# The norms of a four-layer graph kernel: who adds epsilon, who takes the power, who makes the shift

## The chip, the cores and the metric

The kernel runs on one core of one Trainium2 chip. The metric is device microseconds of one launch. A run of the kernel as it stands takes 2153.46 us in the median of three runs (2152.71 to 2155.54). The program's instructions are written out at compile time; nothing in their order is decided on the chip.

## What is computed

There are 128 graphs of 64 nodes with 256 features each, and one 64x64 adjacency matrix shared by all of them. Four layers follow each other, and each begins with a norm:

```python
for layer in (L0, L1, L2, L3):
    m = mean(x, -1);  v = var(x, -1)
    h = maximum((x - m) / sqrt(v + 1e-5), 0)
    x = x + layer(h, adj, weights)
```

- L0 has two graph products with a dense layer each, then four LSTMs over windows of 1, 2, 3 and 4 nodes.
- L1 has a graph product, attention with 4 heads of 64, a feed-forward part, and three more norms inside: after the graph product, after the attention and at the end.
- L2 is a graph attention layer. L3 works in the eigenbasis of the normalised Laplacian, so the kernel also decomposes a 64x64 matrix.

## The kernel before

**Tiles.** The 8192 rows (128 graphs of 64 nodes) are 64 tiles of 128 rows. L0 runs in 8 groups of 8 tiles; the other three layers run in 16 groups of 4 tiles (`HT = 4`). Two 64-row graphs share a tile.

**Stages.** In the profile, L0's groups run from the start to about 1360 us, roughly 165 us each; the groups of L1 to L3 run from about 1364 us to the end, with up to eight of them open at once. The decomposition (vectors of 1 to 128 elements in the tile `arena`) runs beside L0 as background work for VectorE until about 1300 us.

**Who sets the order.** No engine's order is written by hand. The class `Plan` (line 69) records every operation, simulates the five engines with a price for each operation (`cost`, line 176), and lists the operations in the order in which the simulation started them (`schedule`, line 227). `issue` (line 338) then emits them, which is why all instructions carry line 344 in the profile. Each engine runs its own list strictly in that order; semaphores make it wait for the other engines. Four facts of the planner matter here:

- The price of a GpSimd power is 0.44 + 0.14 us an element, of other GpSimd work 0.12 + 0.00218 us an element (line 217). VectorE's tensor_scalar between two SBUF tensors is 0.075 + 0.0006 us an element, scalar_tensor_tensor 0.075 + 0.00105.
- Operations that the planner counts as using the port that VectorE and GpSimd share (`op.port`, line 159: all of GpSimd's, and VectorE's that touch SBUF alone, but not bn_stats, bn_aggr and reductions) are never started side by side in the simulation.
- Between ready operations of one engine, `rank` (line 328) decides. In L0, the norms of the next group (`plan.lead = 1`, line 1311) go ahead of the LSTMs of the current one.
- A different price or engine anywhere can change the order everywhere after it.

**The norm.** `ln_stats` (line 1195) takes the statistics of `n` tiles (4, or 2 in the first group): bn_stats and bn_aggr on VectorE for each tile, giving mean and variance, then four small operations on GpSimd for all `n` at once (lines 1204 to 1207): add 1e-5 to the variance, raise to the power -0.5, multiply the mean by that, negate. The results are a scale and a shift per row. ScalarE applies them in one activation per tile, either with a Relu (`relu_norm`, line 1509, and in `layer0`, line 1309) or without (`norm`, line 1498). All these small values live in one tile `stat`.

**How many.** L0 has 4 norms in its first group and 2 in each of the other 7, so 18. L1, L2 and L3 have 6 norms per group of 4 tiles (4 in `layer1`, line 1523, and 1 each in `layer2`, line 1598, and `layer3`, line 1632), and 16 groups, so 96. Together there are 114, which is also the number of powers in the profile.

**Other names.** `big` are 4-tile buffers (parts of `arena`, `sums`, `mids` and `Whh` become `big` buffers once L0 and the decomposition are done). `mids` are the short-lived buffers of L0's gates. `bank` are the eight PSUM banks. `mhalf` holds -0.5.

Of the kernel before, what the change touches and what calls it, by code (L numbers as in the profile page):

```python
# [8 lines left out]
ALU = mybir.AluOpType  # L9
# [923 lines left out]
def gnn_kernel(ctx: ExitStack, tc: tile.TileContext, a, out):  # L933
# [48 lines left out]
    PE, V, ACT, G, SP = (plan.proxy(e) for e in ("PE", "V", "ACT", "G", "SP"))  # L982
# [212 lines left out]
    def ln_stats(src, n=HT):  # L1195

        s = plan.value("stat")
        st = s[:, :6 * n].rearrange("p (t k) -> p t k", k=6)
        mv = s[:, 6 * n:8 * n].rearrange("p (t k) -> p t k", k=2)
        rs = s[:, 8 * n:10 * n].rearrange("p (k t) -> p k t", k=2)  # L1200
        for t in range(n):
            V.bn_stats(st[:, t, :], src[:, t, :])
            V.bn_aggr(mv[:, t, :], st[:, t, :])
        G.tensor_scalar(rs[:, 0, :], mv[:, :, 1], 1e-5, None, op0=ALU.add)
        G.tensor_tensor(rs[:, 0, :], rs[:, 0, :], mhalf[:, :n], op=ALU.pow)
        G.tensor_tensor(rs[:, 1, :], mv[:, :, 0], rs[:, 0, :], op=ALU.mult)
        G.tensor_scalar(rs[:, 1, :], rs[:, 1, :], -1.0, None, op0=ALU.mult)
        return lambda t: rs[:, 0, t:t + 1], lambda t: rs[:, 1, t:t + 1]


# [98 lines left out]
    def layer0(fetched):  # L1309
        x = fetched()  # L1310
        plan.lead = 1
        nl = 2 if plan.group == 0 else HT
        norms = [ln_stats(x[t // HT][:, t % HT:t % HT + nl, :], nl) for t in range(0, GT, nl)]
        ayT = [fm() for hf in range(2)]
        for t0 in range(0, GT, nl):
# [182 lines left out]
    def norm(t):  # L1498

        sc, bi = ln_stats(t)  # L1500
        for i in range(HT):
            ACT.activation(t[:, i, :], t[:, i, :], AF.Identity, scale=sc(i), bias=bi(i))
# [6 lines left out]
    def relu_norm(x):  # L1509
        sc, bi = ln_stats(x)  # L1510
        h = tm()
        for t in range(HT):
            ACT.activation(h[:, t, :], x[:, t, :], AF.Relu, scale=sc(t), bias=bi(t))
        return h
# [197 lines left out]
```

## Time and profile before

| what | value |
|---|---|
| median of three runs | 2153.46 us |
| the profiled execution's own time | 2151.09 us |
| span of that execution, first to last instruction | 2149.3 us |
| TensorE busy in the span | 2102.0 us (98%) |
| VectorE busy | 1796.7 us (84%), 7434 instructions |
| ScalarE busy | 1124.1 us (52%) |
| GpSimd busy | 708.4 us (33%), 1040 instructions |
| the 114 powers on GpSimd | 123.9 us, 1088 ns each |
| the 228 adds and negations beside them | 69.8 us, 307 ns each |
| the 114 multiplications, nearly all of them (110) | 28.8 us, 264 ns each |

Between the profiled execution's span and its own time lie 1.8 us. The profile calls the engines PE (TensorE), DVE (VectorE), ACT (ScalarE), POOL (GpSimd) and SP (the queue that starts transfers). Busy times are sums over the whole launch. As the stages differ much, the views by stretch of time tell more than the totals.

### The profile page before, as it was taken

What the parts mean: (1) busy time and instruction counts of PE and PEld (TensorE: products, weight loads), DVE (VectorE), ACT (ScalarE), POOL (GpSimd) and SP (SyncE); (2) the same over time, 40 slices, a digit from 0 to 9 for tenths busy, and PEclk for the clock granted to TensorE, in tenths of its full rate; (3) what the DMA queues carried; (4) which work ended last, traced back from release to release, by engine and by line L of the source; (5) the groups of instructions that cost most, each with busy time, mean ns of one, the idle gap of its engine ahead of it and who ended that gap; (6) DMA issues with size and microseconds to landing.
All of it is one profiled execution on the core that took longest, in us unless ns stands there. A gap on an engine that the chain in (4) does not pass through costs nothing.

```text
span 2149.3 us, 46200 instructions
## 1 busy us (share of the span) xinstructions
PE 2102.0 (98%) x16772; PEld 1665.0 (77%) x16772; DVE 1796.7 (84%) x7434; ACT 1124.1 (52%) x2465; POOL 708.4 (33%) x1040
## 2 busy tenths in 40 slices
PE   9999999999999999999999999999999999999998
PEld 6688688688778778778778788877777877887776
DVE  5788888888999999989989898767787789876787
ACT  3354354355345345345345444566667666665783
POOL 7211211310110110110110002696556657864353
PEclk9999999999999999999999999999999999999999
DMA  5000100100100100100000111200000100000001
GB/s 206 1 3 22 42 2 22 41 1 21 40 1 21 40 1 21 40 1 21 26 1 21 50 40 51 90 1 2 21 22 21 41 22 21 11 12 11 2 2 60
DMA packets 44868, 57.70 MB, mean 27 GB/s; under 512 B 8928, under 2 KB 38496, under 8 KB 44640
## 3 DMA queue, kind: packets, MB, share of 16 engines
q1 hardware_dynamic: 43536, 53.71, 7.6%
q8 instruction: 131, 2.15, 0.4%
q10 hardware_dynamic: 1104, 1.05, 0.2%
q14 instruction: 97, 0.79, 0.1%
HBM read 37.53 MB, written 16.78 MB: 25 GB/s over the span
## 4 chain that ended last, share of the span: by engine, by line
PE 79%; DVE 11%; POOL 3%; issue 3%; ACT 2%; DMA 2%; SPq 0%; DVEq 0%; ACTq 0%; POOLq 0%
PE bank L344 79%; DVE stat L344 3%; DVE arena L344 3%; DVE big L344 3%; POOL stat L344 2%; DVE mids L344 1%; DVE sums L344 1%; DMA big<-in_x_dram 1%; ACT big L344 1%; ACT mids L344 1%; POOL arena L344 0%; ACT arena L344 0%; POOL big L344 0%; DVE Whh L344 0%; SPq L344 0%
## 5 line engine op out<-in xcount | busy, mean ns | idle before, releaser
L344 PE MATMUL bank<-big,Wih 128*128 128x256 f32 (+3 forms) x2408 | 731.7, 426 | 14.7 <-DVE arena L344 6.9
L344 PEld LDWEIGHTS bank<-big,Wih 128*128 128x128 f32 x2408 | 440.3, 190 | 183.0 <-issue 100.2
L344 ACT ACTIVATE mids<-bank,bl 128x256 f32<-128x256 f32 (+3 forms) x528 | 274.8, 527 | 385.7 <-PE bank L344 383.3
L344 PE MATMUL bank<-big,Whh 128*128 128x256 f32 (+2 forms) x1692 | 448.0, 366 | 1.5 <-DVE big L344 1.4
L344 DVE TENSOR_TENSOR arena<-arena 64x21 f32<-64x21 f32 (+5 forms) x2253 | 372.3, 195 | 29.5 <-POOL arena L344 1.2
L344 PEld LDWEIGHTS bank<-big,Whh 128*128 128x128 f32 x1692 | 306.8, 190 | 40.6 <-issue 8.6
L344 PE MATMUL bank<-big,sums 128*128 128x168 f32 (+2 forms) x1472 | 263.8, 321 | 1.6 <-ACT big L344 1.5
L344 POOL TENSOR_SCALAR stat<-stat 128x4 f32<-128x4 f32 (+1 forms) x228 | 69.8, 307 | 514.0 <-DVE stat L344 499.2
L344 PEld LDWEIGHTS bank<-big,sums 128*128 128x128 f32 (+1 forms) x1472 | 220.5, 185 | 17.4 <-issue 3.4
L344 ACT COPY mids<-bank 128x168 f32<-128x168 f32 (+2 forms) x427 | 146.2, 364 | 151.9 <-PE bank L344 146.0
L344 DVE TENSOR_TENSOR big<-mids 128x512 f32<-128x512 f32 (+2 forms) x256 | 141.5, 562 | 33.9 <-ACT mids L344 30.7
L344 ACT ACTIVATE mids<-mids,bl 128x336 f32<-128x336 f32 (+3 forms) x192 | 102.1, 539 | 78.7 <-DVE mids L344 74.9
L344 DVE TENSOR_TENSOR mids<-bank,mids 128x168 f32<-128x168 f32 (+2 forms) x322 | 116.1, 368 | 25.1 <-PE bank L344 17.6
L344 DVE SCALAR_TENSOR_TENSOR arena<-arena 64x1 f32<-64x1 f32 (+15 forms) x565 | 124.3, 243 | 6.1 <-POOL arena L344 2.5
L344 POOL TENSOR_TENSOR stat<-stat,mhalf 128x4 f32<-128x4 f32 (+1 forms) x114 | 123.9, 1088 | 5.6
L344 ACT ACTIVATE mids<-big 128x256 f32<-128x256 f32 (+2 forms) x176 | 89.4, 510 | 62.7 <-DVE big L344 46.3
L344 POOL TENSOR_TENSOR big<-big 128x168 f32<-128x168 f32 (+1 forms) x30 | 21.4, 726 | 272.5 <-DVE arena L344 105.7
L344 DVE TENSOR_SCALAR arena<-arena 64x1 f32<-64x1 f32 (+8 forms) x533 | 102.4, 199 | 8.3 <-POOL arena L344 0.4
L344 DVE TENSOR_TENSOR big<-big,mids 128x256 f32<-128x256 f32 (+2 forms) x194 | 95.2, 492 | 9.7 <-ACT mids L344 8.5
L344 PE MATMUL bank<-Wih,big 128*128 128x256 f32 x384 | 94.1, 383 | 3.1 <-DVE big L344 0.9
L344 POOL TENSOR_TENSOR arena<-arena 64x1 f32<-64x1 f32 (+1 forms) x70 | 46.8, 669 | 145.9 <-ACT arena L344 105.8
L344 ACT ACT_TABLE_LOAD x55 | 70.6, 1283 | 35.9 <-PE bank L344 18.0
(371 smaller groups left out, 3747.9 us busy)
## 6 DMA issues: line engine op xcount, KB each, us to landing
big<-in_x_dram SPq DMA_DIRECT2D x30, 512.0 KB, 5.5
put<-big SPq DMA_DIRECT2D x16, 512.0 KB, 2.8
arena<-put SPq DMA_DIRECT2D x8, 512.0 KB, 6.6
out_dram<-arena SPq DMA_DIRECT2D x16, 256.0 KB, 2.3
Wih<-in_WihT_dram SPq DMA_DIRECT2D x3, 1024.0 KB, 11.9
Whh<-in_WhhT_dram SPq DMA_DIRECT2D x3, 1024.0 KB, 13.9
big<-put SPq DMA_DIRECT2D x5, 512.0 KB, 5.4
out_dram<-big SPq DMA_DIRECT2D x10, 256.0 KB, 2.2
```

The costliest lines, as they stand in the source:

```text
L344: getattr(self.engines[op.eng], name)(*map(real, args), **{k: real(a) for k, a in kw.items()})
```

## The change

In `ln_stats`, epsilon is added by VectorE, the power stays on GpSimd, and the shift is made by one VectorE operation, (mean x -1) x scale, in place of a multiplication and a negation on GpSimd.

```diff
         for t in range(n):
             V.bn_stats(st[:, t, :], src[:, t, :])
             V.bn_aggr(mv[:, t, :], st[:, t, :])
-        G.tensor_scalar(rs[:, 0, :], mv[:, :, 1], 1e-5, None, op0=ALU.add)
+        V.tensor_scalar(rs[:, 0, :], mv[:, :, 1], 1e-5, None, op0=ALU.add)
         G.tensor_tensor(rs[:, 0, :], rs[:, 0, :], mhalf[:, :n], op=ALU.pow)
-        G.tensor_tensor(rs[:, 1, :], mv[:, :, 0], rs[:, 0, :], op=ALU.mult)
-        G.tensor_scalar(rs[:, 1, :], rs[:, 1, :], -1.0, None, op0=ALU.mult)
+        V.scalar_tensor_tensor(rs[:, 1, :], mv[:, :, 0], -1.0, rs[:, 0, :], op0=ALU.mult, op1=ALU.mult)
         return lambda t: rs[:, 0, t:t + 1], lambda t: rs[:, 1, t:t + 1]
```

The way from statistics to scale and shift was VectorE, GpSimd, ScalarE. It is now VectorE, GpSimd, VectorE, ScalarE, so VectorE's list holds an operation that waits for GpSimd. As the planner prices the new operations differently, it may put everything in another order.

## The prediction

> **What bounds the kernel now.** I read the shares of the engines first, then the busy times by stretch, then who TensorE waits for, and last the instructions around the places where it waits.
>
> ```profile
> PE 2102.0 (98%) x16772; PEld 1665.0 (77%) x16772; DVE 1796.7 (84%) x7434; ACT 1124.1 (52%) x2465; POOL 708.4 (33%) x1040
> ```
>
> TensorE lacks only 2149.3 - 2102.0 = 47 us of the span. By stretch (columns: stretch, length, then busy time and count of PE, PEld, DVE, ACT, POOL):
>
> ```profile
> 600.00:900.00 300.00, 296.11 (x1619) 237.60 (x1620) 279.87 (x1269) 137.69 (x312) 28.91 (x44) 1.00 0.07 22
> ...
> 1700.00:1900.00 200.00, 197.00 (x2217) 157.15 (x2216) 168.22 (x479) 137.85 (x257) 136.03 (x178) 1.00 0.06 18
> ...
> 2100.00:2149.30 49.30, 39.39 (x671) 33.38 (x669) 34.23 (x103) 17.79 (x35) 17.65 (x25) 0.97 0.16 55
> ```
>
> In the first layer VectorE is 93% busy and GpSimd 10%; later VectorE is at 84% and GpSimd at 68%; only in the last 50 us does TensorE stand for 10 us. So no gain of more than a few us is to be had but at the ends. The waits of TensorE from 60 to 1222 us:
>
> ```profile
> PE bank L344 <- DVE arena L344: 5.5, 5, 1.4
> PE bank L344 <- ACT mids L344: 2.7, 1, 2.7
> PE bank L344 <- DVE big L344: 2.2, 1, 2.2
> ```
>
> These 10.4 us are nearly all at six places, where one group of layer 0 ends and the next begins (227, 396, 563, 726, 890, 1052 us; 2.19, 1.41, 1.21, 1.21, 2.69, 1.21 us, sum 9.9). The fourth, from the timeline:
>
> ```profile
> 727.81 0.16 DVE L344 BATCH_NORM_AGGREGATE stat<-stat 128x2 f32<-128x6 f32 x1
> ...
> 728.06 0.23 POOL L344 TENSOR_SCALAR stat<-stat 128x4 f32<-128x4 f32 x1 [96.30 <-DVE stat L344]
> ...
> 728.37 1.04 POOL L344 TENSOR_TENSOR stat<-stat,mhalf 128x4 f32<-128x4 f32 x1
> ...
> 728.99 0.29 DVE L344 BATCH_NORM_AGGREGATE stat<-stat 128x2 f32<-128x6 f32 x2
> 729.20 1.26 DVE L344 TENSOR_TENSOR big<-mids 128x512 f32<-128x512 f32 x2
> ...
> 730.58 2.08 ACT L344 ACTIVATE mids<-big,stat 128x256 f32<-128x256 f32 x4
> 730.60 3.67 PE L344 MATMUL bank<-big,Wih 128*128 128x512 f32 x8 [1.21 <-DVE arena L344]
> ...
> 734.20 1.16 PE L344 MATMUL bank<-adjTb,mids 64*64 64x64 f32 x64
> ```
>
> The page blames "DVE arena", but what I read is this: VectorE spends 3.2 us on 8 bn_stats and 8 bn_aggr of the coming norms, and only then, at 729.20, makes the two LSTM products that give the gate buffers back; TensorE starts 0.14 us after they end (730.46). The norm's own user, the matmuls at 734.20, has no gap before it. At this place VectorE's time is dear and the norm's speed is worth nothing.
>
> **What the Trainium skill says.** "SBUF — State Buffer", section "Who interferes with whom": VectorE and GpSimd share a port pair; a VectorE instruction with two SBUF inputs, or a tensor_scalar in a two-port mode, and a GpSimd instruction block each other, whichever starts second waiting. Both new instructions are of these kinds. The trace agrees for VectorE: a tensor_scalar of 128x256 took 0.93 us at 2083.03, while GpSimd's 1.27 us addition from 2082.54 ran, and 0.28 us at 2102.96 with GpSimd idle. "TensorE: Matmul & The Clock Gate", section "Architectural detail: the array is 16× 32×32, not 1× 128×128", calls VectorE's queue strict FIFO: what waits at its head holds all behind it. The trace has no reordering on VectorE, but no wait for a norm's power in great number either, so it can't show the cost.
>
> **The change, part by part.** Each of 114 norms (18 in layer 0, 96 later) loses three GpSimd operations and gains two VectorE ones.
>
> *GpSimd.* Removed are 69.8 us of tensor_scalar (228) and about 30 us of multiplication (114 x 0.264): 100 of 708 us. Off TensorE's path, so worth nothing by itself.
>
> *VectorE's own time.* 4-element operations are not in the trace in these forms; the nearest rows are tensor_scalar 64x6 at 166 ns and scalar_tensor_tensor 64x1 at 189 ns. Back to back they take less: a bn_aggr of 155 ns lets the next start after 0.08 us, a dependent one follows after about 0.19 us (64x6 rows near 1228 us). So 0.08 to 0.19 us each; I take 0.15: 228 x 0.15 = 34 us, 5 of them in layer 0 and 29 later.
>
> *The latency of a norm.* Undisturbed, as at 2132 us, aggregation ends at 2132.01, the power starts at 2132.42, the negation ends at 2134.05: 2.04 us. After: eps add 0.17, hand-over 0.09 (as the aggregation at 6.75 to the addition at 6.84), power 1.04, hand-over 0.1, shift 0.19, hand-over as now: 1.6 to 1.7, so 0.35 saved. Where GpSimd is loaded, other additions now stand between power and negation (the median from the power's start to the negation's end is 1.88 us over the later layers, often 3 to 4); this too goes.
>
> *The wait.* The shift waits at the head of VectorE's list for the power. Nothing if the planner's clock is right (it prices the power at 1.00; 1.04 undisturbed, 1.10 mean), up to 1.04 us if VectorE arrives with the power just begun, more if GpSimd is behind. Behind it stand LSTM products, evacuations of PSUM, statistics, and so TensorE. The nearest row is layer 1's pass through GpSimd (multiply, add, maximum; 32 times):
>
> ```profile
> DVE sums L344 <- POOL sums L344: 10.6, 2, 9.4
> ...
> DVE sums L344 <- POOL stat L344: 0.9, 1, 0.9
> ```
>
> The first line is that pass, in which alone VectorE waits for such results there: 10.6 us for 32 passes, 0.33 us each, 0.04 without the longest. I take 0.3. (The second, 0.9 us, is all that VectorE waits for GpSimd's small statistics now.)
>
> *Layer 0, six places.* Ahead of the two LSTM products come now two epsilon additions and the first shift: 3 x 0.15 = 0.45 us, plus 0.05 of wait (the power starts about 728.2 and ends at 729.3, when VectorE has just finished the statistics). 6 x 0.5 = +3.0 us. Ends: 3 x 0.08 = 0.24 each, +1.4; and with one full wait of 1.04 each, +8.9; a gain is excluded, since nothing there stands waiting for a norm.
>
> *Later layers.* VectorE gains 29 us of work, 96 x 0.3 = 29 us of waits, and port holds: GpSimd's 128x512 additions take some 250 us of these 779 (a third), and an instruction that meets one waits half of its 1.3 us: 192 x 1/3 x 0.65 = 42 us. Together 100 us on an engine that is now idle for some 160. TensorE's waits put to VectorE from 1370 us to the end sum to 9.9 us, at about 615 us of VectorE work, 1.6%; as the margin shrinks I take 2%: 100 x 0.02 = +2.0 us. Ends: 0 if eight open groups cover it all, +10 if a tenth comes through; a gain, from the shorter latency, is the second rival.
>
> *The ends.* The last group's final three norms lie on the path: 3 x 0.35 = -1.0 us. When layers 1 to 3 begin (1370 to 1393 us), norms of several groups queue on GpSimd; TensorE lacks 1.6 us in 1380 to 1400; I take half, -0.8 us. In the first group transfers until 32 us cover everything: 0. If the last three norms lose their VectorE slot to other work, the -1.0 is gone.
>
> *Sum.* +3.0 + 2.0 - 1.0 - 0.8 = +3.2 us. The profiled execution took 2151.09 us (span 2149.3 and 1.8 around it), so 2154.3; the median is 2.4 higher, so 2153.46 + 3.2 = **2156.7 us**, +0.15%. A difference under 0.2%, 4.3 us, is about what a measurement of this kernel can't tell from none.
>
> **Rivals.**
> - *VectorE is held at its head.* The planner's list is right only while GpSimd keeps its time; under port conflicts powers take up to 1.99 us. A full 1.04 us at the six places (+8.9) and +4 later, less 1.8 at the ends: +11, **2164.6**. It speaks for it that VectorE is at 93% in layer 0, against it the 0.04 us of layer 1's usual pass. It decides where shifts wait over 0.5 us on average.
> - *The norms get faster, and it shows* (the other side). In the later layers a norm waits through GpSimd's list, and ScalarE waits 86 us there for it. If the shorter list closes half of the 25 us that TensorE lacks after 1370 us, -12, and layer 0 and VectorE's load cost +5: -7, **2146.5**. Against it: of these 25 us the trace puts only 0.8 directly to a norm on GpSimd. It decides where the stretch after 1370 us gains more than layer 0 loses.
> - *Nothing.* The new order happens to hide the added work at the six places: +0.5, **2154.0**.
>
> **Chances.** The sum's case 58% (own range 2152.5 to 2161.5: 30 points within 0.2%, 28 slower, as a new order moves it by some us either way), held VectorE 20% (slower), faster norms 16% (14 faster, 2 within), nothing 6% (within). Together 14% faster, 38% within, 48% slower. The range is 2149 to 2168: up to the held case and its spread, down to the upper half of the faster one; it leaves out about 2 in 10.
>
> **What would show it.** Right: TensorE's gaps at the six places longer by 0.3 to 0.6 us each, GpSimd about 100 us less busy, VectorE some 30 us more, waits of VectorE for "POOL stat" of 20 to 40 us where there were 0.9, aggregation to activation near 1.7 us at the last norm. Wrong: gaps at the six places unchanged, or TensorE's lack after 1370 us changed by over 5 us.

## The result, and the profile after

| | before | after |
|---|---|---|
| median of four runs each | 2153.54 us (2152.71 to 2155.54) | 2176.02 us (2175.23 to 2180.85) |
| ratio | | 1.0108, 95% interval 1.0094 to 1.0122 |
| the profiled execution's own time, and its span | 2151.09, 2149.3 us | 2175.5, 2173.7 us |

The change costs 22.5 us, 1.1%. The forecast was +3.2 us, with a range up to 2168: the sign of the likeliest case was right, the size was not. The page's shares of the engines, after:

```profile
PE 2103.6 (97%) x16772; PEld 1667.0 (77%) x16772; DVE 1837.8 (85%) x7662; ACT 1107.9 (51%) x2449; POOL 614.6 (28%) x698
```

GpSimd lost 93.8 us of work (about 100 were foreseen) and VectorE gained 41.1 (some 30 were). TensorE's work is unchanged (2103.6 against 2102.0), but it lacks 70.1 us of the span where it lacked 47.3. So the loss is standing time of TensorE. By stretch (columns as before; behind the engines stand the granted TensorE clock as a share of full speed, the busy share of the DMA engines and their GB/s):

```profile
600.00:900.00 300.00, 295.37 (x1613) 237.02 (x1611) 278.76 (x1275) 134.74 (x307) 20.26 (x28) 1.00 0.06 20
1700.00:1900.00 200.00, 189.85 (x2111) 151.16 (x2113) 174.53 (x530) 135.20 (x250) 110.72 (x98) 1.00 0.07 21
2100.00:2173.70 73.70, 59.75 (x1019) 50.67 (x1017) 56.82 (x195) 34.16 (x65) 22.17 (x20) 0.99 0.13 45
```

From 1700 to 1900 us TensorE lacks 10.2 us where it lacked 3.0, although VectorE is only at 87% there and GpSimd less busy than before.

**A cut that divides the loss.** The first transfer that belongs to the later layers (the profile shows it on SP's queue as arena<-put) starts at 1364.56 us before and at 1377.08 after. Up to it, both kernels do exactly the same matmuls, 8136. The busy times up to the cut, before and after (columns as above):

```profile
0.00:1364.56 1364.56, 1342.42 (x8136) 1061.76 (x8137) 1178.72 (x5666) 610.36 (x1515) 228.82 (x401) 1.00 0.09 29
```

```profile
0.00:1377.08 1377.08, 1344.29 (x8136) 1061.79 (x8137) 1187.80 (x5706) 610.98 (x1515) 209.60 (x341) 1.00 0.09 29
```

Layer 0 is 12.5 us longer: 10.7 of them TensorE stands (32.8 against 22.1), and 1.9 it spends on the same matmuls. The rest of the span is 796.6 us where it was 784.7, 11.9 longer, all of it standing. (The two make 24.4 us and not 22.5, since the profiled execution before lies 2.4 us under its median.) Layer 0 has 18 of the 114 norms and more than half of the loss, so the loss doesn't follow the number of norms.

**The first group.** From the timeline, the start before. The first norm is complete at 8.7 us and the first graph product starts at 9.38:

```profile
6.84 0.24 POOL L344 TENSOR_SCALAR stat<-stat 128x2 f32<-128x2 f32 x1 [4.84 <-DVE stat L344]
...
7.17 0.73 POOL L344 TENSOR_TENSOR stat<-stat,mhalf 128x2 f32<-128x2 f32 x1
...
8.72 1.09 ACT L344 ACTIVATE mids<-big,stat 128x256 f32<-128x256 f32 x2 [3.87 <-POOL stat L344]
...
9.38 1.41 PE L344 MATMUL bank<-adjTb,mids 64*64 64x64 f32 x32 [1.93 <-ACT mids L344]
```

And after:

```profile
8.49 0.43 DVE L344 BATCH_NORM_STATS2 stat<-big 128x6 f32<-128x256 f32 x1 [0.51 <-DMA big<-in_x_dram]
...
9.70 0.35 DVE L344 TENSOR_SCALAR stat<-stat 128x2 f32<-128x2 f32 x4
9.93 2.91 POOL L344 TENSOR_TENSOR stat<-stat,mhalf 128x2 f32<-128x2 f32 x4 [6.88 <-DVE stat L344]
...
12.96 0.15 DVE L344 SCALAR_TENSOR_TENSOR stat<-stat 128x2 f32<-128x2 f32 x1
...
13.15 2.57 ACT L344 ACTIVATE mids<-big,stat 128x256 f32<-128x256 f32 x5 [8.38 <-DVE stat L344]
...
13.80 2.50 PE L344 MATMUL bank<-adjTb,mids 64*64 64x64 f32 x68 [0.95 <-ACT mids L344]
```

The four epsilon additions ("x4" at 9.70) come together, behind the statistics of all eight tiles, and one of these waits for an input transfer. The first shift comes only at 12.96, and TensorE starts its first graph product 4.4 us later.

**The fourth of the six places**, where VectorE's list was thought to delay the two LSTM products:

```profile
734.40 0.67 DVE L344 TENSOR_TENSOR big<-mids 128x512 f32<-128x512 f32 x1
...
735.01 0.73 DVE L344 BATCH_NORM_STATS2 stat<-big 128x6 f32<-128x256 f32 x2
...
735.23 3.24 PE L344 MATMUL bank<-big,Wih 128*128 128x512 f32 x7 [1.56 <-DVE big L344]
```

The product now stands ahead of the statistics, so no addition and no shift can delay it, and still TensorE waits 1.56 us there (1.21 before) and another 1.40 at 742. This isn't the old order with two operations more; it is another order. Compared as lists, the matmuls of the two kernels differ from the first graph product on: 6609 of 16772 stand at the same place.

### The profile page after: what moved, and what is told of

The parts are those of the page before. It is cut to its first block, busy times and chain, and to the rows that moved or that the text cites. A ratio compares the mean times of both kernels' runs of the same rounds, so it can differ in the third digit from the quotient of the medians.

```text
span 2173.7 us, 45985 instructions
## 1 busy us (share of the span) xinstructions
PE 2103.6 (97%) x16772; PEld 1667.0 (77%) x16772; DVE 1837.8 (85%) x7662; ACT 1107.9 (51%) x2449; POOL 614.6 (28%) x698
## 4 chain that ended last, share of the span: by engine, by line
PE 80%; DVE 14%; DMA 2%; ACT 2%; issue 1%; POOL 1%; SPq 0%; DVEq 0%; ACTq 0%; POOLq 0%
PE bank L344 80%; DVE stat L344 4%; DVE arena L344 4%; DVE big L344 3%; DVE mids L344 2%; DVE sums L344 1%; DMA big<-in_x_dram 1%; ACT sums L344 0%; ACT big L344 0%; SPq L344 0%; POOL big L344 0%; ACT mids L344 0%; DMA Whh<-in_L_b_dram 0%; DMA arena<-put 0%; DMA Wg<-in_Wg_dram 0%
## 5 line engine op out<-in xcount | busy, mean ns | idle before, releaser
L344 PE MATMUL bank<-big,Wih 128*128 128x256 f32 (+3 forms) x2408 | 731.9, 426 | 19.1 <-DVE arena L344 10.7
L344 PE MATMUL bank<-big,Whh 128*128 128x256 f32 (+3 forms) x1948 | 452.7, 347 | 1.8 <-DVE big L344 1.7
L344 PEld LDWEIGHTS bank<-big,Whh 128*128 128x128 f32 (+1 forms) x1948 | 311.1, 183 | 40.6 <-issue 7.4
L344 POOL TENSOR_TENSOR stat<-stat,mhalf 128x4 f32<-128x4 f32 (+1 forms) x114 | 130.5, 1150 | 453.1 <-DVE stat L344 448.2
L344 PEld LDWEIGHTS bank<-big,sums 128*128 128x128 f32 (+1 forms) x1536 | 221.9, 183 | 15.8 <-issue 2.6
L344 ACT COPY mids<-bank 128x168 f32<-128x168 f32 (+2 forms) x400 | 131.7, 351 | 149.2 <-PE bank L344 145.9
L344 ACT ACTIVATE mids<-mids,bl 128x336 f32<-128x336 f32 (+2 forms) x192 | 102.1, 539 | 74.2 <-DVE mids L344 71.3
L344 PE MATMUL bank<-Wih,big 128*128 128x256 f32 x448 | 112.6, 386 | 6.4 <-ACT big L344 3.2
L344 ACT COPY big<-bank 128x512 f32<-128x512 f32 (+1 forms) x148 | 70.7, 506 | 63.9 <-PE bank L344 63.1
L344 PEld LDWEIGHTS bank<-Wih,big 128*128 128x128 f32 x448 | 82.5, 192 | 23.2 <-issue 4.6
L344 PE MATMUL bank<-Wih,sums 128*128 128x256 f32 x312 | 78.8, 388 | 5.4 <-ACT sums L344 2.7
## 6 DMA issues: line engine op xcount, KB each, us to landing
Wih<-in_WihT_dram SPq DMA_DIRECT2D x3, 1024.0 KB, 11.9
Whh<-in_WhhT_dram SPq DMA_DIRECT2D x3, 1024.0 KB, 13.9
```

The lines of the kernel that those rows point to most:

```text
L344: getattr(self.engines[op.eng], name)(*map(real, args), **{k: real(a) for k, a in kw.items()})
```

## The experiments

Three questions were put in turn: operations or order; where the order loses; and whether the order alone is enough. Each kernel ran beside the kernel before on the same chip, at 2153.4 to 2154.1 us in the median. "Standing" is TensorE's lack of busy time in the profiled span. Some expectations speak of the planner's own clock: that is the span with which its simulation ends, worked out as the program is compiled, and no measurement.

### Operations or order

**The new engines in the old order.** The planner records the four old operations and orders them as before; only when they are written out are the first and the last two replaced.

```diff
-                for name, args, kw in op.calls:
-                    getattr(self.engines[op.eng], name)(...)
+                for eng, name, args, kw in getattr(op, "emit", [(op.eng, *c) for c in op.calls]):
+                    getattr(self.engines[eng], name)(...)
...
         G.tensor_scalar(rs[:, 0, :], mv[:, :, 1], 1e-5, None, op0=ALU.add)
+        plan.ops[-1].emit = [("V", *plan.ops[-1].calls[0])]
         G.tensor_tensor(rs[:, 0, :], rs[:, 0, :], mhalf[:, :n], op=ALU.pow)
         G.tensor_tensor(rs[:, 1, :], mv[:, :, 0], rs[:, 0, :], op=ALU.mult)
+        plan.ops[-1].emit = []
         G.tensor_scalar(rs[:, 1, :], rs[:, 1, :], -1.0, None, op0=ALU.mult)
+        plan.ops[-1].emit = [("V", "scalar_tensor_tensor", ...)]
```

> The order is planned as before the change, with four GpSimd operations at their old prices; only when it is written out does the epsilon addition go to VectorE, at the addition's place in the order, and the shift as one VectorE operation, at the negation's place. The lists of TensorE, ScalarE and the DMA queue are those of before. If the two VectorE operations cost time by themselves (VectorE standing for the power, port holds), this is as slow as the change: 2170 to 2178 us. If the loss is that the planner wrote another order, it lies at 2150 to 2158 us. If both share it, 2160 to 2168 us.

Measured: 2162.96 us, ratio 1.0048 (1.0033 to 1.0063), +9.2. The profiled execution is its slowest, +13.8. Its VectorE stands 18.7 us in 20 waits for powers (total, times, longest):

```profile
DVE stat L344 <- POOL stat L344: 18.7, 20, 2.1
```

**The new order with the old engines.** The reverse: the planner orders the changed operations, and the old ones are written out (addition on GpSimd, and GpSimd's multiplication and negation in the place of the shift).

```diff
         V.tensor_scalar(rs[:, 0, :], mv[:, :, 1], 1e-5, None, op0=ALU.add)
+        plan.ops[-1].emit = [("G", *plan.ops[-1].calls[0])]
...
         V.scalar_tensor_tensor(...)
+        plan.ops[-1].emit = [("G", "tensor_tensor", ...), ("G", "tensor_scalar", ...)]
```

> The order is planned as after the change, but the epsilon addition is written out on GpSimd at its place, and at the place of the shift stand the multiplication and the negation on GpSimd. If the VectorE operations cost time by themselves, this falls back to 2150 to 2158 us, a few us more for GpSimd's operations standing where VectorE's were planned. If the other order is the loss, it stays at 2168 to 2178 us. If both share it, 2160 to 2168 us.

Measured: 2176.93 us, ratio 1.0109 (1.0092 to 1.0126), +23.2. All work is where it was before, and the whole loss is there. Its cut lies at 1376.05 us:

```profile
0.00:1376.05 1376.05, 1345.76 (x8136) 1064.91 (x8137) 1178.55 (x5666) 610.00 (x1515) 227.55 (x401) 1.00 0.09 29
```

The counts of VectorE and GpSimd (x5666, x401) are those of the kernel before; TensorE stands 30.3 us, as after the change (32.8). Its first graph product comes at 12.44 us, so the late start follows the order too. The order is enough to make the loss. The old operations stand here at places planned for others, though, and how much of the 23.2 us that adds isn't known.

**Each half in the old order.** Only the addition, or only the shift, is moved when written out (the first, or the last two, of the three lines above).

> In the order planned before the change, only the epsilon addition is written out on VectorE. If the direct loss of 9 us in the old order is VectorE's standing for the power and the port holds of the shift, this is 2153 to 2156 us. If VectorE's place for the addition (behind statistics that wait for a transfer, or held by GpSimd's port) is the loss, 2158 to 2163 us.

> In the order planned before the change, only the shift is written out on VectorE, at the negation's place. If VectorE's standing for the power and the port holds of the shift are the direct loss, 2159 to 2164 us. If the addition is, 2153 to 2156 us.

Measured: 2159.2 us (1.0029, 1.0016 to 1.0042) and 2159.25 us (1.0028, 1.0018 to 1.0038), +5.4 and +5.5. The halves together, 10.9, are about the 9.2 of both. Only the second waits at VectorE's head for powers, 21.1 us in 17 waits; the addition, which waits for nothing new on its own engine, costs as much in the median, though its runs spread from 2154.7 to 2162.3 us (mean granted clock 0.998 and 0.993).

**Each half, planned anew.** The change with the old multiplication and negation, and the change with the old addition.

> Only the epsilon addition goes to VectorE, planned anew; the shift stays two GpSimd operations, so VectorE never waits for a power. If the wait of the shift at the head of VectorE's list is the loss, 2152 to 2158 us. If VectorE's late epsilon additions hold back the first group, about 4 us of loss are here, 2157 us. If a new order as such is the loss, anything from 2155 to 2178 us.

> Only the shift goes to VectorE, planned anew; epsilon stays on GpSimd. If the wait of the shift at the head of VectorE's list and its port holds are the loss, nearly all of it is here: 2168 to 2176 us. If the epsilon addition is what hurts, 2152 to 2158 us. If a new order as such is the loss, anything from 2155 to 2178 us, with no sum to be made of this and the addition alone.

Measured: 2178.49 us (1.0117, 1.0102 to 1.0133) and 2183.28 us (1.0144, 1.0129 to 1.0159). The shift alone costs more than both together; the addition alone costs about as much as both, as the two intervals overlap. Both lie above 2178 us, the most that was expected of a new order. No sum over operations can give that.

### Where the order loses

**A nudge of one price.** In the kernel before, one number of the planner is changed, and no operation.

```diff
-            c = 0.44 + 0.14 * n if op.kw.get("op") is ALU.pow else 0.12 + 0.00218 * n
+            c = 0.44 + 0.14 * n if op.kw.get("op") is ALU.pow else 0.121 + 0.00218 * n
```

The second has 0.119 there; the third has 0.45 for 0.44 at the power. The fourth is the change with 0.45 for 0.44.

> The kernel before, in which the planner's fixed price of a GpSimd operation other than the power is 0.121 us in place of 0.120; no operation changes. If the order before was a lucky one and any new order costs about 1%, this takes 2165 to 2180 us. If the loss comes from where the change's own prices lead the planner, it stays within 2148 to 2160 us.

> The kernel before with that price at 0.119 us; no operation changes. As for 0.121: 2165 to 2180 us if any new order costs about 1%, 2148 to 2160 us if the change's own prices are to blame.

> The kernel before with the planner's price of a power 0.45 + 0.14 us an element in place of 0.44; no operation changes. 2165 to 2180 us if any new order costs about 1%, 2148 to 2160 us if the change's own prices are to blame.

> The changed kernel with the planner's price of a power 0.45 + 0.14 us an element. If orders differ by luck, this is another draw and may lie anywhere from 2158 to 2185 us. If the change's place in the order makes the loss, it stays at 2172 to 2180 us.

Measured: +10.9 us (1.0049, 1.0029 to 1.0069), +5.4 (1.0027, 1.0015 to 1.0039) and +9.4 (1.0043, 1.0023 to 1.0063); the change nudged is at 2176.38 us (1.0107, 1.0071 to 1.0143), where it was. A thousandth of a microsecond in one price can cost as much as both new operations in the old order. But the three medians lie between 2159.4 and 2165.0 us: the "about 1%" expected of any new order is 0.3 to 0.5% here. The nudged kernels' cut lies at 1365.2, 1369.2 and 1365.3 us (1364.6 before), and the rest is 12.6, 3.7 and 12.1 us longer. So a nudge can make the whole loss of the later layers, but none comes near layer 0's +12.5, which needs another cause.

**Layer 0 alone, the later layers alone.** The change under `if plan.group < REST`, and under `>=`.

> Only the 18 norms of layer 0 are changed, planned anew. The transfer of the first later group starts at 1364.6 us before the change and at 1377.1 after it. If that loss is layer 0's own, it stays: the transfer starts at 1375 to 1378 us, and with the later part as before the whole takes 2163 to 2168 us. If it needs the later norms, about 2155 us.

> Only the 96 norms of the later layers are changed, planned anew. If the two halves of the loss are separate, the transfer starts near 1365 us and the whole takes 2163 to 2168 us, and the two halves sum to the change's 22 us. If one half alone carries it, this lies at 2154 or at 2176 us.

Measured: 2160.55 us (1.0034, 1.0022 to 1.0046), +6.8, and 2172.71 us (1.0087, 1.0072 to 1.0102), +18.9. Both miss the ranges expected, and the two losses sum to 25.7 us where the change costs 22.5. In the first the cut lies at 1373.76 us and the rest is 784.7 us long, exactly as before. In the second the rest is 16.1 us longer, and layer 0 is 5.3 longer although no norm in it is changed. Of these, 3.1 us are no matter of order: up to 1283 us the matmuls come in the same sequence as before, and the delay is made in two steps, near 235 and 896 us, where the granted clock fell to half in this execution. The second step, and the same stretch before:

```profile
896.45:899.87 3.42, 3.42 (x5) 1.35 (x4) 3.25 (x13) 1.70 (x4) 3.17 (x5) 0.50 0.13 43
```

```profile
896.45:899.87 3.42, 3.42 (x9) 1.28 (x7) 3.25 (x14) 2.62 (x6) 3.17 (x6) 1.00 0.00 0
```

So a few us of layer 0 between two single executions can be the clock. The nudged kernel with its cut at 1369.2 us has 2.5 of its 4.6 in the same way.

**The first group's four norms alone** (`if plan.group == 0`).

> Only the four norms of layer 0's first group are changed. If layer 0's loss comes from that group's late epsilon additions: the first transfer of the later layers starts about 8 to 9 us later than before (near 1373 us), the later part is as long as before, and the time is 2159 to 2162 us. If it comes from the six places between groups: the start moves by less than 3 us and the time is 2153 to 2157 us.

Measured: 2160.8 us, ratio 1.0035 (1.0022 to 1.0048), +7.2; the rest of the span after the cut is 784.8 us. Up to the cut:

```profile
0.00:1374.38 1374.38, 1344.29 (x8136) 1061.46 (x8137) 1179.59 (x5674) 611.19 (x1515) 224.70 (x389) 1.00 0.09 29
```

+9.8 us, of which 8.0 standing and 1.9 busy. Four norms out of 18 make all that layer 0 loses by itself; changing the other fourteen too (+9.2) adds nothing. And its six places, where no operation is changed, sum to 12.1 us of gaps against 9.9: they move with the order. (By the medians of the launch it is +7.2 us for four norms and +6.8 for eighteen.)

**The change without the planner's port rule for the two new operations.** Their `op.port` is set to false, so that they may be started beside GpSimd's work in the simulation.

> The change in full, but the planner no longer counts the two new operations as users of the port that VectorE and GpSimd share, so that it may start them beside GpSimd's work. If the late start comes from that rule: the first matmul of the first group starts by 10 us instead of 13.8. If the rule owns layer 0's loss, the later layers then begin 4 us earlier or more than after the change (by 1373 us). The order theory for the total: the planner's clock gives 2158.7 us, as for the change, so 2172 to 2178 us. The rival, that the rule owns most of the loss: 2160 to 2168 us.

Measured: 2182.04 us, ratio 1.0134 (1.0119 to 1.015). The rule does own the late start: the first product of the graph now begins at 9.60 us.

```profile
6.52 0.15 DVE L347 TENSOR_SCALAR stat<-stat 128x2 f32<-128x2 f32 x1
...
6.75 0.72 POOL L347 TENSOR_TENSOR stat<-stat,mhalf 128x2 f32<-128x2 f32 x1 [4.47 <-DVE stat L347]
...
9.60 3.65 PE L347 MATMUL bank<-adjTb,mids 64*64 64x64 f32 x96 [2.65 <-ACT mids L347]
```

But the total was expected between 2172 and 2178 us and is 4 us above that, and the cut moves only 1.5 us:

```profile
0.00:1375.59 1375.59, 1350.01 (x8136) 1064.20 (x8137) 1189.59 (x5706) 611.01 (x1515) 212.90 (x341) 0.99 0.09 29
```

Standing in layer 0 falls from 32.8 to 25.6 us, but the same 8136 matmuls now take 1350.0 us in place of 1344.3: a lower granted clock (0.99) takes most of it back. The launch's first stretch at half clock ends no earlier for the earlier start, so more matmuls fall into it (after the change, then without the rule):

```profile
8.36:18.60 10.24, 5.27 (x101) 4.47 (x102) 5.31 (x39) 5.45 (x14) 6.86 (x8) 0.50 0.92 316
```

```profile
8.53:18.77 10.24, 9.05 (x110) 7.54 (x111) 6.00 (x36) 5.63 (x14) 4.28 (x7) 0.50 0.92 310
```

Later in layer 0 the clock is at half for three more stretches of 3.41 us without the rule (from 233.8, 739.0 and 1066.7 us), and for one after the change (from 1066.5). As an estimate from these figures, matmuls at half clock lose half of their busy time: half of the 3.8 us more in the first stretch and of the two stretches more after it is 5.3 of the 5.7 us. So the late start explains TensorE's 4.0 us more of standing in the first 60 us (they are gone without the rule), and a repair of it was not a repair of layer 0.

### Is the order enough by itself?

**Other prices, operations unchanged, and other prices with the change.** Three numbers in the planner differ. The diff is that of the first kernel; the second has 0.1165, 0.494 and 0.17 in their places, so the two are no pair.

```diff
-            return c, c + 0.12
+            return c, c + 0.127
...
-            c = 0.44 + 0.14 * n if op.kw.get("op") is ALU.pow else 0.12 + 0.00218 * n
+            c = 0.466 + 0.14 * n if op.kw.get("op") is ALU.pow else 0.118 + 0.00218 * n
```

> No operation differs from the kernel before. Three prices in the planner do: GpSimd 0.118 for 0.12 at its base, 0.466 for 0.44 for the power, VectorE's latency 0.127 for 0.12. The planner's own clock gives this order 2168 us, against 2138 before and 2159 with the change. The order theory: the time follows the order, so 2168 + 16 = 2184 us (2178 to 2190), slower than the change though not one operation is changed. The rival, that nearly all of the change's loss beyond a nudge's 5 to 11 us belongs to its operations: a repriced order costs what the nudges cost, 2159 to 2166 us.

> The change in full, with three other prices in the planner: GpSimd 0.17 for 0.12 at its base, 0.494 for 0.44 for the power, VectorE's latency 0.1165 for 0.12. The planner's own clock gives 2152.8 us, against 2158.6 for the change at the old prices. The order theory: 2168 us (2163 to 2172), between the change and the kernel before, and still not below the 2163 us that the changed operations take in the old order. The rival, that the operations themselves cost what the change costs: within 3 us of 2176.

Measured: 2191.6 us, ratio 1.0177 (1.0162 to 1.0192), +38 with no operation changed; and 2167.9 us, ratio 1.0066 (1.0049 to 1.0083), 8 below the change at the old prices. The first is even above its expectation. Its profile shows what a bad order is. The busy times from 1372 to 1500 us, and the place there where TensorE waits longest:

```profile
1372.00:1500.00 128.00, 103.53 (x1208) 83.83 (x1212) 94.16 (x276) 68.15 (x138) 90.98 (x120) 0.88 0.01 4
```

```profile
1460.42 2.05 PE L344 MATMUL bank<-ident,big 128*128 128x128 f32 x8 [8.19 <-DVE big L344]
```

TensorE stands 24.5 of these 128 us (6.5 before), with every other engine busy less than 75%. In the longest wait, though, VectorE is busy throughout:

```profile
1452.23:1460.42 8.19, 0.00 (x1) 0.01 (x1) 8.19 (x32) 0.00 (x0) 3.54 (x6) 0.80 0.00 0
```

```profile
1459.69 0.68 DVE L344 SCALAR_TENSOR_TENSOR big<-big,sums 128x512 f32<-128x512 f32 x1
```

This last operation is what TensorE waits for. By the planner's clock it was ready 7.6 us before its turn, but `rank` put the statistics of twelve tiles of later groups ahead of it. So it is the list that leaves TensorE without work, by what comes first on an engine that has room over the whole stretch.

**A pair at the same prices.** The setting that, among 40 random ones, gave the changed operations the shortest span by the planner's clock; with the change, and without it.

> The change in full, at the prices which, of 40 random settings close to the old ones, gave the changed operations the shortest span by the planner's own clock: GpSimd 0.1199 for 0.12 at its base, 0.438 for 0.44 for the power, VectorE's latency 0.1245 for 0.12. The clock gives 2149.3 us, of which layer 0 is 1367.6. The order theory: 2149.3 + 16 = 2165 us (2161 to 2169), 11 below the change at the old prices. If its operations had a fixed cost of 22 us: 2173 to 2179.

> The operations of the kernel before at the same prices as same_prices_changed. The planner's clock gives 2150.5 us, of which layer 0 is 1365.3. The order theory: 2166 us (2162 to 2171), so that at these prices the kernel with the change and the one without it take the same time within 4 us. If the change's operations cost 22 us in any order, this one is some 20 us below same_prices_changed.

Measured: 2170.68 us (1.0077, 1.0065 to 1.009) and 2169.18 us (1.0078, 1.0065 to 1.0092). The two intervals lie on each other. In this pair, where both are planned anew, the change costs nothing that can be seen. But the setting was picked as the best of 40 for the changed operations; in other settings the clock puts the changed kernel up to 30 us above the unchanged one, or 17 below it. The changed one missed its own expectation, 2161 to 2169 us, by 2.

| kernel | planner's clock, us | measured, us |
|---|---|---|
| before | 2137.8 | 2153.5 |
| before, same other prices as the pair | 2150.5 | 2169.2 |
| before, other prices | 2168.1 | 2191.6 |
| the change | 2158.6 | 2176.0 |
| the change, the pair's prices | 2149.3 | 2170.7 |
| the change, its own other prices | 2152.8 | 2167.9 |
| the change, no port rule | 2158.7 | 2182.0 |

The chip takes 15 to 24 us more than the clock in these rows. Over all 16 kernels with a plan of their own it is 11 (the nudge down) to 25 us (the later layers alone), so the clock tells orders apart to some 7 us. Over the 40 settings it has a median of 2150 us for the old operations and 2160 for the changed; only one of the 40 lies below the kernel before. So by the clock, which is an estimate and no measurement, leaving the old order costs 12 us whatever the operations, and the changed operations cost 10 more in a usual setting. The pair doesn't show these 10. No version beat the kernel before.

## Why the prediction was wrong

**The replanning was the step that failed.** The prediction knew that another order would come, and gave it "some us either way". Measured, every new plan is slower: three nudges cost 5.4 to 10.9 us, other prices 15.8 and 38, and the change's own order 23.2 with no operation moved. The old order was an unusually good one for this planner, so nearly any edit that makes it plan again starts from a loss. The same holds inside the sum: each term was worked out as an operation put into, or taken from, a list that otherwise stays.

**"In the first group transfers until 32 us cover everything: 0".** This is the step with a fixed place, and it failed: with these four norms alone changed, layer 0 is 9.8 us longer and the launch 7.2. TensorE is not covered there: before, it is busy 55.0 of the first 60 us, a stretch that the prediction's table left out when it found TensorE standing "only in the last 50 us". I had read transfers in flight as a wait of TensorE, and had not asked which norm lets TensorE start.

**Six places, +3.0.** The gaps grew from 9.9 to 14.4 us, +4.5, but not for the reason given. In the old order with both operations on VectorE they sum to 10.5, so the operations cost 0.5 there, and a first-group edit far away moved them by 2.2. At the fourth place in the old order a single addition stands ahead of the products and delays them by 0.06 us from start to start:

```profile
731.39 0.14 DVE L344 TENSOR_SCALAR stat<-stat 128x4 f32<-128x4 f32 x1
731.45 0.17 DVE L344 BATCH_NORM_AGGREGATE stat<-stat 128x2 f32<-128x6 f32 x1
...
732.45 1.26 DVE L344 TENSOR_TENSOR big<-mids 128x512 f32<-128x512 f32 x2
...
733.86 2.38 PE L344 MATMUL bank<-big,Wih 128*128 128x512 f32 x5 [1.27 <-ACT mids L344]
```

I had put three operations of 0.15 us ahead of them.

**Later layers, +2.0.** VectorE's load was overrated and its effect underrated. After the cut its work grew by 32.0 us (650.0 against 618.0), port holds included, and its shifts waited 9.9 us for powers: 42 in place of the 100 in the sum. Yet the stretch after the cut is 9.8 us longer in the old order and 11.9 in the new. The rate of 2% failed: TensorE's share of waits put to VectorE says how often it came last, not what a delay does to a list in which eight groups follow each other.

**The operations' own sizes** held: GpSimd -93.8 us (100 foreseen), and each new instruction near 0.15 us:

```profile
L344 DVE TENSOR_SCALAR stat<-stat x114: 108/160/1242, 9.7 to 2156.6; 128x4 f32<-128x4 f32 x110, 128x2 f32<-128x2 f32 x4
...
L344 DVE SCALAR_TENSOR_TENSOR stat<-stat x114: 103/152/1249, 13.0 to 2158.3; 128x4 f32<-128x4 f32 x110, 128x2 f32<-128x2 f32 x4
```

The columns after the count are minimum, median and maximum in ns. The waits of VectorE for powers were priced at 29 us in the later layers. There they are 9.9, in the whole launch 13.9 (us, times, longest):

```profile
DVE stat L344 <- POOL stat L344: 13.9, 16, 2.1
```

The Trainium skill's page "TensorE: Matmul & The Clock Gate", section "Architectural detail: the array is 16× 32×32, not 1× 128×128", calls VectorE's queue strict FIFO; the 18.7 us of the old order are such waits, and the 13.9, with the waits known to the planner, are fewer.

**The ends, -1.8.** Little came of it. At the last norm, the aggregation ends at 2156.60 us and the shift at 2158.41, 1.81 us where it was 2.04: 0.23 saved, not 0.35. The shift had its power at 2157.91, but on VectorE's list two products stood before it:

```profile
2156.89 1.02 POOL L344 TENSOR_TENSOR stat<-stat,mhalf 128x4 f32<-128x4 f32 x1 [6.56 <-DVE stat L344]
...
2157.06 1.29 DVE L344 TENSOR_TENSOR sums<-bank,sums 128x512 f32<-128x512 f32 x2 [0.25 <-PE bank L344]
...
2158.26 0.15 DVE L344 SCALAR_TENSOR_TENSOR stat<-stat 128x4 f32<-128x4 f32 x1
2158.51 2.08 ACT L344 ACTIVATE big<-arena,stat 128x256 f32<-128x256 f32 x4 [6.63 <-DVE stat L344]
```

From 1372 to 1500 us, where 0.8 was to be gained, TensorE stands 9.1 us in place of 6.5.

**The rivals.** "VectorE is held at its head" gave 2164.6, near the 2162.96 of the old order, but it was to decide from 0.5 us a shift; measured are 18.7 / 114 = 0.16, and the addition alone, which isn't held so, costs as much. "Faster norms" and "nothing" fell. None of the four cases had the new order itself as a cost; "nothing" had it as a help. Of the signs named beforehand, one of being wrong came true: TensorE's lack after 1370 us was to change by no more than 5 us, and after the cut it grew by 12.1 (37.3 against 25.2).

**What stays open.** How much of the 22.5 us the operations own has no single answer: 9.2 in the old order, nothing in the new order (2176.0 with them, 2176.9 without), nothing in the pair, and about 10 in the middle of 40 settings by the planner's clock. Why the order after the change lacks 7 us more between 1700 and 1900 us was not traced to one decision of the planner. A norm with fewer operations and all of it on GpSimd was not tried.

## What to carry to other kernels

Where a compile-time planner orders the work, an edit has two costs: its instructions in the list as it stands, and the new list. Measure the second by itself, with nudges of a price that change no operation: an edit that moves the time by no more than they do can't be told from a new list. One kernel before and one after, both planned anew, aren't enough either, where plans of the same operations differ by as much as 38 us. And at a launch's start, ask what lets the busiest engine begin: four norms there cost 7 us here, in an order that put their additions last.

## What the runs showed of the hardware

**Tiny instructions are held as long as big ones.** "SBUF — State Buffer", section "Who interferes with whom", says that the later of two instructions waits for the shared port. Here a shift of four elements a row, 0.15 us by itself, took 1.21 us beside two GpSimd additions, and ends at 1858.86, right after the first of these (1858.84):

```profile
1857.14 2.93 POOL L344 TENSOR_TENSOR sums<-sums,Wih 128x512 f32<-128x512 f32 x2
...
1857.65 1.21 DVE L344 SCALAR_TENSOR_TENSOR stat<-stat 128x4 f32<-128x4 f32 x1
```

Of the 228 new instructions 31 took over 0.25 us (24 shifts and 7 additions), 25.6 us together, and a GpSimd instruction ran beside each of them; the prediction's 42 us of holds took no account of the planner's port rule.

**A gap costs twice.** Soon after the sixth place's gap of 3.29 us, which ends at 1065.37, the granted clock is half for 3.41 us (the column before the last two):

```profile
1066.49:1069.90 3.41, 3.41 (x12) 0.91 (x15) 3.18 (x14) 2.53 (x6) 2.22 (x4) 0.50 0.00 0
```

Before, a gap of 2.69 us left it at 1.00:

```profile
890.00:900.00 10.00, 7.31 (x21) 2.84 (x22) 9.78 (x36) 6.62 (x12) 7.28 (x12) 1.00 0.54 175
```

In other kernels here gaps of 2.47 and 2.86 us lowered it too, and one of 2.92 did not; at the first place a gap of 2.19 us did in one execution (only the later layers changed) and did not in another (before), with the same matmuls in the same sequence. So for gaps of 2 to 3 us it can go either way. "TensorE: Matmul & The Clock Gate", section "What's actually happening", has the clock fall after an idle window of about 3.4 us; the runs show it from shorter gaps as well. This and the start at half clock are why layer 0's time without the port rule hardly fell with its standing time.
